# A causal attention and gated FFN layer: K's rows stored once and read through two overlapping windows, and another order for the opening

## The chip, the cores and the metric

The kernel runs on one core of a Trainium2 chip. The metric is the time of one execution in device microseconds. A core has TensorE (PE) for matrix products, VectorE (DVE), ScalarE (ACT) and GpSimd (POOL) for the rest, a sync engine (SP) that only issues transfers here, and 16 DMA engines that carry out what SP, ACT and POOL issue, each through a queue of its own. Data lies in DRAM, in SBUF (128 partitions) or in PSUM, where TensorE writes.

## The reference

Input x is 4096 tokens of 256 features in float32. The layer is attention with its own input norm, a residual and a norm, then the FFN, a residual and a norm:

```python
# attention: 16 heads of 16, causal
xn = (x - mean) * rsqrt(var + 1e-5) * gamma + beta
q, k, v = split(xn @ w_qkv.T)               # w_qkv: (768, 256)
sim = (q * 16**-0.5) @ k.T                  # per head, 4096 x 4096
sim = where(causal_mask, -max, sim)
out = softmax(sim) @ v
x = layernorm(x + out)
# FFN: ternary weights times a scale per output feature
h = silu((x @ w1.T) * s1) * ((x @ w2.T) * s2)    # 256 -> 1024
h = gelu((h @ h1.T) * t1)                        # 1024 -> 1024
h = gelu((h @ h2.T) * t2)                        # 1024 -> 1024
x = layernorm(x + (h @ w3.T) * s3)               # 1024 -> 256
```

## The kernel before

Tokens come in 8 blocks of 512 (`NB`, `B`), heads in 4 groups of four (`NQ`). Precision is kept by splitting: a value is a high part, rounded to the fast format of TensorE, and a low part, the rest. A product of two split values takes high times high, low times high and high times low.

**Projections** (`projections`, L200). For each block of tokens: load x (`fetch`), normalize it, transpose it on TensorE (`front`, L214), split it in xh and xl, and project K, Q and V with the split weights wh and wl, 12 matmuls of 512 columns for K, 12 for Q, 24 of 256 columns for V. The result of K or Q is a tile of 128 output features by 2 by 512 tokens. ACT copies its high part (kh, L263), DVE makes the low part (kl, L265), and both are stored to DRAM (L269): `kaug` and `qaug` hold, for each head, the 16 rows of a part one above another. The tuple `order` says which part goes into each group of 16: K is stored as high, high, low and Q as high, low, high, so that a single product over 48 rows gives the three terms. Two rows of ones (L274) follow in kaug; against them stand, in Q's tile, two rows with the high and low part of the negative row maximum. For block 0 the stores are dealt over the queues of ACT, SP and POOL, for the others they are all POOL's. V goes to `vaug` with a column of ones, which later gives the row sums.

**Attention** (`layer`, L296). Work goes by steps of a query block and a head group. For each step there are two passes over the key blocks up to the diagonal. `row_max` (L425) multiplies Q by K and reduces the maximum of each row on DVE (L453). `rows` (L458) turns these maxima into two rows of Q's tile (qt<-hl, L469). `scores` (L476) multiplies K by Q with all 50 rows, so that the maximum comes off in the product, and ACT takes the exponential (L490). `product` (L500) multiplies V by it; `divide` divides by the row sums and stores the step's output to `attn`.

K is read again for each step and each pass. `fetch(kind, key)` (L401) loads a K tile from kaug, kind "m" (mk) for the maxima, kind "s" (sk, with V in vk) for the scores. Two of each exist, and a tile is asked for one ahead. A K tile takes two loads on SP (L410), half e for partitions 64e to 64e+49, each with two heads side by side:

```python
hs = slice(4 * qd + e, 4 * qd + 4, 2)
nc.sync.dma_start(
    kt[half * e : half * e + KR].bitcast(F32), self.kaug[kb][hs].rearrange("r p t -> p r t")
)
```

**The order of the work.** Each engine's compute instructions run in the order in which the program writes them (`in_order`). A planner writes it: `ahead` gives the row maxima, `behind` the scores; a score step is written when the maxima are `lead` units of work ahead, where `lead` is the size of the current step plus `extra`, and a unit is a quarter of a K tile. After every two or three of them, `other` writes a pair of products, a piece of the projections, or a piece of the FFN. Blocks 0 and 1 are projected before the first step (`FIRST` is 2), the others in between. When all are projected and a query block is finished, its FFN starts (`start`, `feed`): load x and attn, add them, normalize, and run the three layers in pieces with their weights loaded by POOL. The last block's FFN has no attention beside it and comes at the end (`closing`). `scales` loads the FFN's scale vectors, and computes two products of them on POOL; it is called once before the first step.

Of the kernel before, what the change touches and what calls it, by code (L numbers as in the profile page):

```python
# [46 lines left out]

class Layer:
    def __init__(self, tc, a):
        self.tc, self.nc, self.a = tc, tc.nc, a  # L50
        self.last = {}

# [28 lines left out]

    def run(self):
        tc, nc, a = self.tc, self.nc, self.a
        with ExitStack() as ctx:
            dram = self.pool(ctx, "dram", space=DRAM)
            cst = self.pool(ctx, "cst")
            self.small = self.pool(ctx, "small", 4)
            self.qaug = [dram.tile([H, 48, B], F32, name=f"qaug{b}") for b in range(NB)]
            self.kaug = [dram.tile([H, KR, B], F32, name=f"kaug{b}") for b in range(NB)]
            self.vaug = [dram.tile([NQ, P, 4, 4, D + 1], F32, name=f"vaug{b}") for b in range(NB)]  # L90
            self.attn = [dram.tile([B, E], F32, name=f"attn{b}") for b in range(NB)]

# [24 lines left out]
    def scales(self):  # L117
        for n, t in self.sc.items():
            self.nc.sync.dma_start(t, self.a[n].rearrange("(c p) -> p c", p=P))
        self.nc.gpsimd.tensor_scalar(self.w1_half, self.sc["w1_s"], 0.5, None, ALU.mult)  # L120
        self.nc.gpsimd.tensor_tensor(self.w12, self.w1_half, self.sc["w2_s"], ALU.mult)
        s3 = self.a["w3_s"].rearrange("(o f) -> o f", o=1)
        self.nc.sync.dma_start(self.s3, s3.broadcast_to([P, E]))

# [75 lines left out]
    def projections(self, ctx):  # L200
# [7 lines left out]

        def fetch(b):
            xb = wk.tile([P, 4, E], F32, name="xb")  # L210
            nc.sync.dma_start(xb, tokens(a["x"][b * B : (b + 1) * B]))
            return xb

        def front(b, xb):  # L214
            xn = wk.tile([P, 2, B], F32, name="xn", bufs=1)
            for c in range(2):
# [22 lines left out]
        self.layernorm(xb, xb)  # L239
        yield from front(0, xb)  # L240
        xb = ahead
        wh = one.tile([P, 2, 3 * E], FR, name="wh")
        nc.vector.tensor_copy(wh, w)
        wl = one.tile([P, 2, 3 * E], FR, name="wl")
        nc.vector.tensor_tensor(wl, w, wh.bitcast(F32), ALU.subtract)
# [5 lines left out]
        self.layernorm(xb, xb)  # L251
        for b in range(NB):
            xh, xl = parts.pop(b)
            prods = [(wh, xh, c) for c in range(2)] + [(wl, xh, c) for c in range(2)] + [(wh, xl, c) for c in range(2)]
            for off, dst, order in ((E, self.kaug, (0, 0, 1)), (0, self.qaug, (0, 1, 0))):
# [7 lines left out]
                nc.scalar.copy(kh, kp)  # L263
                kl = wk.tile([P, 2, B], FR, name="kl")
                nc.vector.tensor_tensor(kl, kp, kh.bitcast(F32), ALU.subtract)  # L265
                for n, (i, g) in enumerate(sorted((i, g) for g, i in enumerate(order))):
                    for T in range(2):
                        queues = (nc.scalar, nc.sync, nc.gpsimd) if b == 0 else (nc.gpsimd,)
                        queues[(2 * n + T) % len(queues)].dma_start(  # L269
                            dst[b][8 * T : 8 * T + 8, 16 * g : 16 * g + 16, :], (kh, kl)[i][:, T].bitcast(F32)  # L270
                        )
# [24 lines left out]
    def layer(self, ctx):  # L296
# [95 lines left out]
        self.scales()  # L392
# [8 lines left out]
        def fetch(kind, key):  # L401
# [3 lines left out]
            while loaded[kind] < min(j + 2, len(seq)) and seq[loaded[kind]][2] <= self.projected:  # L405
                qb, qd, kb = nxt = seq[loaded[kind]]
                kt = (mk if kind == "m" else sk).tile([P, 2, B], FR, name=kind + "k")
                for e in range(2):
                    hs = slice(4 * qd + e, 4 * qd + 4, 2)
                    nc.sync.dma_start(  # L410
                        kt[half * e : half * e + KR].bitcast(F32), self.kaug[kb][hs].rearrange("r p t -> p r t")
                    )
# [6 lines left out]
                tiles[kind, nxt] = kt, vt  # L419
                loaded[kind] += 1  # L420
# [4 lines left out]
        def row_max(qb, qd):  # L425
            qt = qtile[qb, qd] = qp.tile([P, 2, B], FR, name="qt")
            for e in range(2):
                hs = slice(4 * qd + e, 4 * qd + 4, 2)
                nc.sync.dma_start(
                    qt[half * e : half * e + 48].bitcast(F32), self.qaug[qb][hs].rearrange("r p t -> p r t")  # L430
# [238 lines left out]
    def load(self, b):  # L669
        self.live += 1  # L670
        x1 = self.fk.tile([P, 4, E], F32, name="x1", bufs=3)
        self.nc.sync.dma_start(x1, tokens(self.a["x"][b * B : (b + 1) * B]))
        return x1

    def start(self, b):
# [405 lines left out]
```

## Time and profile before

| | before |
|---|---|
| median of 3 runs | 2464.67 us (2457.7 to 2467.17) |
| the profiled execution | 2476.85 us |
| its span | 2475.1 us |
| mean granted clock of TensorE | 0.933 |
| PE, DVE, ACT, POOL busy | 91%, 63%, 56%, 29% |
| DMA | 310.02 MB in 251,811 packets |

The profile is one execution. It gives, for each engine, the time in which its instructions ran, in total, in 40 slices of the span and by groups of instructions; a group's row names the line, the engine, the operation and its tiles, how often and how long it ran, and what ended the idle time before it. The queue rows count packets: a packet is a piece of a transfer that one DMA engine moves, or a 4-byte completion that it writes when its part of a transfer is done. A window's row gives busy time of PE, PE's weight load, DVE, ACT and POOL, then the granted clock, the mean share of time in which the 16 DMA engines were busy, and GB/s. The chain of waits follows what ended last back to what released it. SPq is SP's queue of issued transfers; in a timeline the second number is how long an issue took.

### The profile page before, as it was taken

The page shows a single profiled execution, that of the slowest core. Times are in us where ns is not written, and L with a number is a line of the kernel's source. Part 1 is how long each engine was busy: PE and PEld are TensorE (multiplying, and loading weights), DVE is VectorE, ACT ScalarE, POOL GpSimd, SP SyncE. Part 2 cuts the span into 40 slices and gives each one's busy share as a digit, 9 for nine tenths or more (in the row PEclk, how much of TensorE's full clock was granted, in tenths as well). Part 3 has the DMA queues.
Part 4 walks back from the last instruction along what each step waited for, and adds up shares of the span by engine and source line. Part 5 has one row for each costly group of instructions (what it writes and reads, how often), then busy time and mean ns, then how long its engine had stood idle before and what let it go on. Part 6 is the DMA issues. An engine that isn't in the chain of part 4 may idle for free.

```text
span 2475.1 us, 36371 instructions
## 1 busy us (share of the span) xinstructions
PE 2259.4 (91%) x13986; PEld 1216.6 (49%) x13986; DVE 1567.3 (63%) x1826; ACT 1394.0 (56%) x1698; POOL 714.2 (29%) x1021
## 2 busy tenths in 40 slices
PE   4677899999998999999899999999999999999888
PEld 3545444545455544545445544554445443454366
DVE  3445687566656667576766677666766467755553
ACT  2242556545655566556665666566666677656731
POOL 2342413143223143131423132131423131313421
PEclk8687889969999989989999989999899999999999
DMA  7776834434643634535354544545354533454933
GB/s 185 200 175 158 192 101 116 121 80 121 128 111 92 156 103 108 129 97 141 103 123 109 139 95 105 132 109 139 80 127 111 142 108 101 110 111 131 243 94 86
DMA packets 251811, 310.02 MB, mean 125 GB/s; under 512 B 41328, under 2 KB 179696, under 8 KB 251632
## 3 DMA queue, kind: packets, MB, share of 16 engines
q1 hardware_dynamic: 141920, 184.87, 26.9%
q0 software_dynamic: 108352, 120.91, 22.6%
q8 instruction: 113, 1.85, 0.3%
q10 hardware_dynamic: 1360, 1.84, 0.2%
q14 instruction: 66, 0.54, 0.1%
HBM read 268.45 MB, written 38.54 MB: 124 GB/s over the span
## 4 chain that ended last, share of the span: by engine, by line
PE 67%; DVE 16%; ACT 7%; DMA 5%; issue 3%; POOL 2%; SPq 0%; ACTq 0%; POOLq 0%; DVEq 0%
PE m L830 17%; PE opsum L504 15%; PE s L486 11%; DVE mp L453 11%; PE s L442 10%; PE m L802 4%; ACT p L490 4%; PE bank L931 2%; PE m L857 2%; PE s L259 2%; PE s L449 1%; DMA qt<-hl 1%; DVE th L806 1%; ACT th L805 1%; DMA mk<-h2T_in 1%
## 5 line engine op out<-in xcount | busy, mean ns | idle before, releaser
L453 DVE TENSOR_REDUCE mp<-s 128x2 f32<-128x1024 f32 (+3 forms) x1152 | 1265.4, 1132 | 560.6 <-PE s L442 404.6
L490 ACT ACTIVATE p<-s 128x1024 f32<-128x1024 f32 (+3 forms) x1152 | 1062.9, 954 | 677.1 <-PE s L486 665.6
L486 PE MATMUL s<-qt,sk 50*128 50x512 f32 (+3 forms) x2304 | 514.6, 452 | 86.2 <-DVE mp L453 46.4
L442 PE MATMUL s<-mk,qt 48*128 48x512 f32 (+3 forms) x2304 | 513.9, 448 | 57.1 <-DVE mp L453 18.4
L504 PE MATMUL opsum<-p,vk 128*17 128x512 f32 (+3 forms) x4608 | 557.0, 586 | 2.8 <-POOL p L493 2.6
L830 PE MATMUL m<-act,wt 128*128 128x512 f32 x1792 | 477.1, 408 | 0.7 <-DVE xl L785 0.7
L486 PEld LDWEIGHTS s<-qt,sk 50*128 50x128 f32 x2304 | 223.1, 193 | 400.5 <-DVE mp L453 141.5
L830 PEld LDWEIGHTS m<-act,wt 128*128 128x128 f32 x1792 | 321.8, 189 | 123.8 <-issue 53.1
L442 PEld LDWEIGHTS s<-mk,qt 48*128 48x128 f32 x2304 | 229.8, 197 | 307.0 <-ACT p L490 134.6
L504 PEld LDWEIGHTS opsum<-p,vk 128*17 128x17 f32 x4608 | 97.7, 98 | 234.1 <-issue 214.1
L493 POOL TENSOR_SCALAR_AFFINE_SELECT p<-p 128x256 f32<-128x256 f32 x256 | 105.1, 420 | 292.1 <-ACT p L490 290.9
L665 POOL DMA_DIRECT2D wt<-h1T_in x64 | 48.9, 764 | 378.9 <-PE m L830 231.0
L665 POOL DMA_DIRECT2D wt<-h2T_in x64 | 49.4, 772 | 366.0 <-PE m L830 310.9
L755 POOL TENSOR_TENSOR act<-raw,act 128x512 fp32r<-128x512 f32 x112 | 145.1, 1295 | 8.9
L838 ACT ACTIVATE raw<-m,h_s 128x512 f32<-128x512 f32 x112 | 77.1, 689 | 107.5 <-PE m L830 107.5
L802 PE MATMUL m<-xh,wt 128*128 128x512 f32 x224 | 105.9, 473 | 11.9 <-DVE th L806 9.1
L449 PEld LDWEIGHTS s<-tri,pick 64*128 64x128 f32 x1024 | 96.1, 205 | 7.2
L802 PE MATMUL m<-xl,wt 128*128 128x512 f32 x224 | 93.3, 416 | 0.0
L449 PE MATMUL s<-tri,pick 64*128 64x128 f32 (+1 forms) x1024 | 88.4, 252 | 0.0
L754 POOL CAST act<-raw 128x512 fp32r<-128x512 f32 x112 | 70.9, 633 | 41.9 <-ACT raw L759 41.9
L754 POOL CAST act<-th 128x512 fp32r<-128x512 f32 x56 | 34.4, 614 | 144.6 <-DVE th L808 144.3
L806 DVE SCALAR_TENSOR_TENSOR th<-th,m 128x512 f32<-128x512 f32 x56 | 38.4, 686 | 55.2 <-ACT th L805 55.1
(126 smaller groups left out, 1530.2 us busy)
## 6 DMA issues: line engine op xcount, KB each, us to landing
mk<-kaug SPq DMA_DIRECT2D x288, 200.0 KB
sk<-kaug SPq DMA_DIRECT2D x288, 200.0 KB
wt<-h1T_in POOLq DMA_DIRECT2D x64, 512.0 KB, 4.3
wt<-h2T_in POOLq DMA_DIRECT2D x64, 512.0 KB, 4.2
vk<-vaug SPq DMA_DIRECT2D x144, 136.0 KB
qt<-qaug SPq DMA_DIRECT2D x64, 192.0 KB
wt<-w1T_in POOLq DMA_DIRECT2D x34, 256.0 KB, 4.2
wt<-w2T_in POOLq DMA_DIRECT2D x34, 256.0 KB, 5.2
```

Source lines behind the costliest of these rows:

```text
L442: nc.tensor.matmul(m[:, e, :k1], qt[rows, r, t * P : (t + 1) * P], kt[rows, r, :k1], start=True, stop=kb != qb,)
L449: nc.tensor.matmul(m[:, e, k1 - P + half * i : k1], pick[rows, i], tri[rows, : P - half * i], start=False, stop=i == 1,)
L453: nc.vector.tensor_reduce(mp[:, r, :, t, kb], m[:, :, :k1], AX.X, ALU.max)
L486: nc.tensor.matmul(s[:, e, lo:], kt[rows, r, t * P : (t + 1) * P], qt[rows, r, lo:], start=True, stop=True)
L490: nc.scalar.activation(p[:, :, lo:], s[:, :, lo:], AF.Exp, scale=0.25)
L493: nc.gpsimd.affine_select(out=p[:, :, lo : lo + P], in_=p[:, :, lo : lo + P], compare_op=ALU.is_ge, fill=0.0, base=0, pattern=[[0, 2], [1, ...
L504: nc.tensor.matmul(opsum[32 * j : 32 * j + D + 1, lo:], vt[:, t, j], pt[j // 2][:, j % 2, lo:], start=first, stop=last,)
L665: self.nc.gpsimd.dma_start(dst, src)
L754: nc.gpsimd.tensor_copy(hi, src)
L755: nc.gpsimd.tensor_tensor(lo, src, hi.bitcast(F32), ALU.subtract)
L802: nc.tensor.matmul(s, wt[:, 2 * i + k, cols], x[:, k], start=k == n == 0, stop=k == n == 1)
L830: nc.tensor.matmul(s, wts[k // 4][:, k % 4, cols], x[:, k % 4], start=k == n == 0, stop=k == 7 and n == 1)
```

## The change

K and Q are stored by dimension: `kaug` becomes 34 rows, each with 16 heads by 512 tokens side by side, `qaug` 48 such rows. K's high part is stored once. Rows 0 to 8 of kaug hold the first 9 rows of the low part, rows 9 to 24 the high part, rows 25 to 31 the rest of the low part, rows 32 and 33 the ones. A load reads rows 0 to 24 and then rows 9 to 33 through an overlapping pattern (`twice`), which gives 50 rows with the high part in them two times; Q's rows are arranged to match. Two heads that share a half of the tile are now neighbours in DRAM, so a row of a load is 4 KB in place of two runs of 2 KB. To get the features of K and Q in this order, their weights are copied by dimension before they are split (`by_dimension`).

The opening changes too. Block 0 of x comes in four loads. The splitting of the weights and the norm steps of blocks 0 and 1 are interleaved in another order. Blocks 0 and 1 are transposed into one PSUM tile of two banks, whose halves ACT and DVE scale. Block 1 is transposed after Q's projection of block 0 in place of K's. Block 0's stores go over the queues of SP and POOL. `scales` is called when the first FFN block starts, and its two products come with that block's addition. `held` orders the loads of x1 and of the scales behind the last K load written so far. `extra` is always 5, where it was 2 for query block 0.

The diff, with what is only declarations left out:

```diff
+KRUNS = ((0, 0, 16, 9), (1, 0, 9, 0), (1, 9, 16, 25))
+QRUNS = ((0, 0, 16, 9), (0, 0, 9, 0), (0, 9, 16, 41), (1, 0, 16, 25))
+
+def twice(ap):
+    dims = [list(d) for d in ap.ap]
+    row = dims[0][0]
+    return bass.AP(ap.tensor, ap.offset, [[9 * row, 2], [row, 25], [1, 2 * B]])
...
+    def held(self):
+        if self.mark:
+            self.after(self.nc.cur_bb.bb.instructions[-1], self.mark)
...
-            self.qaug = [dram.tile([H, 48, B], F32, name=f"qaug{b}") for b in range(NB)]
-            self.kaug = [dram.tile([H, KR, B], F32, name=f"kaug{b}") for b in range(NB)]
+            self.qaug = [dram.tile([48, H, B], F32, name=f"qaug{b}") for b in range(NB)]
+            self.kaug = [dram.tile([34, H, B], F32, name=f"kaug{b}") for b in range(NB)]
...
             self.nc.sync.dma_start(t, self.a[n].rearrange("(c p) -> p c", p=P))
-        self.nc.gpsimd.tensor_scalar(self.w1_half, self.sc["w1_s"], 0.5, None, ALU.mult)
-        self.nc.gpsimd.tensor_tensor(self.w12, self.w1_half, self.sc["w2_s"], ALU.mult)
+            self.held()
...
-            nc.sync.dma_start(xb, tokens(a["x"][b * B : (b + 1) * B]))
+            src = tokens(a["x"][b * B : (b + 1) * B])
+            for ts in [slice(t, t + 1) for t in range(4)] if b == 0 else [slice(0, 4)]:
+                nc.sync.dma_start(xb[:, ts], src[:, ts])
+            loads[b] = nc.cur_bb.bb.instructions[-1].name
...
-            for c in range(2):
+            if b < FIRST:
+                tp = ps.tile([P, 2, B], F32, name="s", tag="s", bufs=3)
+                for t in range(4):
+                    for c in range(2):
+                        nc.tensor.transpose(
+                            tp[:, c, t * P : (t + 1) * P], xb[:, t, c * P : (c + 1) * P], self.ident
+                        )
+                nc.scalar.activation(xn[:, 0], tp[:, 0], AF.Identity, bias=bet[:, 0:1], scale=gam[:, 0:1])
+                nc.vector.tensor_scalar(xn[:, 1], tp[:, 1], gam[:, 1:2], bet[:, 1:2], ALU.mult, ALU.add)
+                yield 8 * TRANSPOSE, True
+            for c in range(2 if b >= FIRST else 0):
...
-        self.layernorm(xb, xb)
+        steps = [step for _, step in self.norm_steps(xb, xb)]
+        for step in steps[:3]:
+            step()
...
+        def by_dimension(copy, off):
+            for k in range(2):
+                for h in range(2):
+                    cs = slice(off + h * P, off + (h + 1) * P)
+                    copy(
+                        wq[:, k, cs].rearrange("p (d q e r) -> p d q e r", d=D, q=2, e=2),
+                        w[:, k, cs].rearrange("p (q r e d) -> p d q e r", d=D, q=2, e=2),
+                    )
+
+        by_dimension(nc.vector.tensor_copy, E)
+        nc.vector.tensor_copy(wh[:, :, E : 2 * E], wq[:, :, E:])
+        for step in steps[3:]:
+            step()
+        by_dimension(nc.scalar.copy, 0)
+        kq = slice(E, 2 * E)
+        nc.vector.tensor_tensor(wl[:, :, kq], wq[:, :, kq], wh[:, :, kq].bitcast(F32), ALU.subtract)
         yield from front(0, xb)
+        for cs, src in ((slice(0, E), wq[:, :, 0:E]), (slice(2 * E, 3 * E), w[:, :, 2 * E :])):
+            nc.vector.tensor_copy(wh[:, :, cs], src)
+            nc.vector.tensor_tensor(wl[:, :, cs], src, wh[:, :, cs].bitcast(F32), ALU.subtract)
...
-                for n, (i, g) in enumerate(sorted((i, g) for g, i in enumerate(order))):
+                for part, d0, d1, row in runs:
                     for T in range(2):
-                        queues = (nc.scalar, nc.sync, nc.gpsimd) if b == 0 else (nc.gpsimd,)
-                        queues[(2 * n + T) % len(queues)].dma_start(
-                            dst[b][8 * T : 8 * T + 8, 16 * g : 16 * g + 16, :], (kh, kl)[i][:, T].bitcast(F32)
+                        queues = (nc.sync, nc.gpsimd) if b == 0 else (nc.gpsimd,)
+                        queues[T % len(queues)].dma_start(
+                            dst[b][row : row + d1 - d0, 8 * T : 8 * T + 8, :],
+                            (kh, kl)[part][8 * d0 : 8 * d1, T].bitcast(F32),
                         )
                 yield 12 * MM, True
                 if dst is self.kaug:
-                    nc.sync.dma_start(self.kaug[b][:, 48:KR, :], ones)
+                    nc.sync.dma_start(self.kaug[b][32:34], ones)
+                    self.after(nc.cur_bb.bb.instructions[-1], loads[b])
+                if dst is (self.kaug if b else self.qaug):
                     if b + 1 < NB:
                         yield from front(b + 1, xb)
...
                 for e in range(2):
-                    hs = slice(4 * qd + e, 4 * qd + 4, 2)
-                    nc.sync.dma_start(
-                        kt[half * e : half * e + KR].bitcast(F32), self.kaug[kb][hs].rearrange("r p t -> p r t")
-                    )
+                    hs = slice(4 * qd + 2 * e, 4 * qd + 2 * e + 2)
+                    nc.sync.dma_start(kt[half * e : half * e + KR].bitcast(F32), twice(self.kaug[kb][:, hs]))
...
+                self.mark = nc.cur_bb.bb.instructions[-1].name
...
-                    qt[half * e : half * e + 48].bitcast(F32), self.qaug[qb][hs].rearrange("r p t -> p r t")
+                    qt[half * e : half * e + 48].bitcast(F32), self.qaug[qb][:, hs].rearrange("p r t -> p (r t)")
...
-                extra = min(EXTRA, 0.8 * size[i])
+                extra = EXTRA
...
+        if b == ORDER[0]:
+            self.scales()
         at = self.fk.tile([P, 4, E], F32, name="at")
...
             nc.gpsimd.tensor_tensor(x1, x1, at, ALU.add)
             self.free("at")
+            if b == ORDER[0]:
+                nc.gpsimd.tensor_scalar(self.w1_half, self.sc["w1_s"], 0.5, None, ALU.mult)
+                nc.gpsimd.tensor_tensor(self.w12, self.w1_half, self.sc["w2_s"], ALU.mult)
```

More of the change, by code (lines that the diff above doesn't have):

```diff
@@ L51, in __init__ @@
         self.last = {}
+        self.mark = None
     def pool(self, ctx, name, bufs=1, **kw):
@@ L119, in scales @@
             self.nc.sync.dma_start(t, self.a[n].rearrange("(c p) -> p c", p=P))
-        self.nc.gpsimd.tensor_scalar(self.w1_half, self.sc["w1_s"], 0.5, None, ALU.mult)
-        self.nc.gpsimd.tensor_tensor(self.w12, self.w1_half, self.sc["w2_s"], ALU.mult)
+            self.held()
         s3 = self.a["w3_s"].rearrange("(o f) -> o f", o=1)
         self.nc.sync.dma_start(self.s3, s3.broadcast_to([P, E]))
+        self.held()
     def norm_steps(self, dst, src):
@@ L207, in projections @@
         wk = self.pool(ctx, "pw", 2, side="right")
+        loads = {}
         def fetch(b):
             xb = wk.tile([P, 4, E], F32, name="xb")
-            nc.sync.dma_start(xb, tokens(a["x"][b * B : (b + 1) * B]))
+            src = tokens(a["x"][b * B : (b + 1) * B])
+            for ts in [slice(t, t + 1) for t in range(4)] if b == 0 else [slice(0, 4)]:
+                nc.sync.dma_start(xb[:, ts], src[:, ts])
+            loads[b] = nc.cur_bb.bb.instructions[-1].name
             return xb
@@ L238, in projections @@
         ahead = fetch(1)
-        self.layernorm(xb, xb)
+        steps = [step for _, step in self.norm_steps(xb, xb)]
+        for step in steps[:3]:
+            step()
+        wq = one.tile([P, 2, 2 * E], F32, name="wq")
+        wh = one.tile([P, 2, 3 * E], FR, name="wh")
+        wl = one.tile([P, 2, 3 * E], FR, name="wl")
+        def by_dimension(copy, off):
[13 more added lines that the diff above has]
+        nc.vector.tensor_tensor(wl[:, :, kq], wq[:, :, kq], wh[:, :, kq].bitcast(F32), ALU.subtract)
         yield from front(0, xb)
+        for cs, src in ((slice(0, E), wq[:, :, 0:E]), (slice(2 * E, 3 * E), w[:, :, 2 * E :])):
+            nc.vector.tensor_copy(wh[:, :, cs], src)
+            nc.vector.tensor_tensor(wl[:, :, cs], src, wh[:, :, cs].bitcast(F32), ALU.subtract)
         xb = ahead
[L242 to L245, printed above, removed]
+        steps = [step for _, step in self.norm_steps(xb, xb)]
+        for step in steps[:4]:
+            step()
         ones = one.tile([32, B], F32, name="ones")
@@ L250, in projections @@
             nc.gpsimd.memset(v, 1.0)
-        self.layernorm(xb, xb)
         for b in range(NB):
@@ L254, in projections @@
             prods = [(wh, xh, c) for c in range(2)] + [(wl, xh, c) for c in range(2)] + [(wh, xl, c) for c in range(2)]
-            for off, dst, order in ((E, self.kaug, (0, 0, 1)), (0, self.qaug, (0, 1, 0))):
+            for off, dst, runs in ((E, self.kaug, KRUNS), (0, self.qaug, QRUNS)):
                 kp = ps.tile([P, 2, B], F32, name="s", tag="s", bufs=3)
@@ L263, in projections @@
                 nc.scalar.copy(kh, kp)
+                if b == 0 and dst is self.kaug:
+                    for step in steps[4:]:
+                        step()
                 kl = wk.tile([P, 2, B], FR, name="kl")
                 nc.vector.tensor_tensor(kl, kp, kh.bitcast(F32), ALU.subtract)
-                for n, (i, g) in enumerate(sorted((i, g) for g, i in enumerate(order))):
+                for part, d0, d1, row in runs:
                     for T in range(2):
-                        queues = (nc.scalar, nc.sync, nc.gpsimd) if b == 0 else (nc.gpsimd,)
-                        queues[(2 * n + T) % len(queues)].dma_start(
-                            dst[b][8 * T : 8 * T + 8, 16 * g : 16 * g + 16, :], (kh, kl)[i][:, T].bitcast(F32)
+                        queues = (nc.sync, nc.gpsimd) if b == 0 else (nc.gpsimd,)
+                        queues[T % len(queues)].dma_start(
+                            dst[b][row : row + d1 - d0, 8 * T : 8 * T + 8, :],
+                            (kh, kl)[part][8 * d0 : 8 * d1, T].bitcast(F32),
                         )
@@ L391, in layer @@
         nc.vector.memset(opsum, 0.0)
-        self.scales()
         steps = [(qb, qd) for qb in ORDER for qd in range(NQ)]
@@ L427, in row_max @@
             for e in range(2):
-                hs = slice(4 * qd + e, 4 * qd + 4, 2)
+                hs = slice(4 * qd + 2 * e, 4 * qd + 2 * e + 2)
                 nc.sync.dma_start(
-                    qt[half * e : half * e + 48].bitcast(F32), self.qaug[qb][hs].rearrange("r p t -> p r t")
+                    qt[half * e : half * e + 48].bitcast(F32), self.qaug[qb][:, hs].rearrange("p r t -> p (r t)")
                 )
@@ L672, in load @@
         self.nc.sync.dma_start(x1, tokens(self.a["x"][b * B : (b + 1) * B]))
+        self.held()
         return x1
```

## The prediction, made before the changed kernel ran

> **What bounds the kernel now.** I read the page first (spans, slices, queues), then the windows table, then what the K tiles wait for, and last the opening as a timeline of SP.
>
> ```profile
> span 2475.1 us, 36371 instructions
> PE 2259.4 (91%) x13986; PEld 1216.6 (49%) x13986; DVE 1567.3 (63%) x1826; ACT 1394.0 (56%) x1698; POOL 714.2 (29%) x1021
> ...
> PE   4677899999998999999899999999999999999888
> ...
> PEclk8687889969999989989999989999899999999999
> DMA  7776834434643634535354544545354533454933
> ```
>
> PE is busy in nine tenths of nearly every slice after the sixth and in 4 to 8 tenths before, at a lower clock. So there are two parts: a body that TensorE bounds, and an opening of about 300 us with room in it.
>
> ```profile
> 300.00:2200.00 1900.00, 1804.56 (x11410) 927.08 (x11406) 1280.18 (x1373) 1153.41 (x1357) 530.01 (x729) 0.95 0.46 114
> 2350.00:2475.00 125.00, 101.98 (x504) 80.21 (x502) 53.36 (x108) 30.96 (x46) 26.89 (x35) 0.93 0.35 89
> ```
>
> From 300 to 2200 us PE is busy 95% at clock 0.95, while the 16 DMA engines are busy 0.46 of the time on average: the transfers are hidden. How well shows in what the score matmuls' tile waited for:
>
> ```profile
>   DMA sk<-kaug: 3.8, 4
> ```
>
> 3.8 us in four waits, in the whole run. Now how those hidden transfers are spread:
>
> ```profile
> q1 hardware_dynamic: 141920, 184.87, 26.9%
> q0 software_dynamic: 108352, 120.91, 22.6%
> ...
> q10 hardware_dynamic: 1360, 1.84, 0.2%
> ...
> mk<-kaug SPq DMA_DIRECT2D x288, 200.0 KB
> sk<-kaug SPq DMA_DIRECT2D x288, 200.0 KB
> vk<-vaug SPq DMA_DIRECT2D x144, 136.0 KB
> qt<-qaug SPq DMA_DIRECT2D x64, 192.0 KB
> ```
>
> K is by far the largest traffic: 576 loads of 200 KB are 118 MB of the 310 MB. A K tile takes two loads (partitions 0 to 49 and 64 to 113), so there are 144 tiles for the maxima (mk) and 144 for the scores (sk), one of each every 2295/144 = 15.9 us between the first load (46 us) and the last (2341 us), and every 14 us in the body.
>
> The opening has one stall to see, on SP:
>
> ```profile
> 46.34 0.33 SPq L410 DMA_DIRECT2D mk<-kaug  x1
> 46.72 3.11 SPq L269 DMA_DIRECT2D qaug<-kl  x1
> 49.88 4.77 SPq L410 DMA_DIRECT2D mk<-kaug  x2
> 62.33 0.96 SPq L429 DMA_DIRECT2D qt<-qaug  x2
> ```
>
> A store of Q's low part stands in SP's order behind a K load that had to wait for K's stores. It leaves at 46.7 though its data was there at about 36; the chain of waits then shows 15.53 us of qaug<-kl and 5.81 us of qt<-qaug, and the first maxima matmul (L442) runs at 67.9 us.
>
> **The change, part by part.**
>
> *The K load.* Before, each load reads 50 rows x 2 heads, 100 runs of 2 KB. After, `twice` reads 2 windows x 25 rows, 50 runs of 4 KB. Bytes and the number of loads stay the same. Packets get longer: in the trace's packet records a 2 KB packet on SP's queue takes 87 ns (median), the 3 KB ones of wqkv 121 ns, the 4 KB ones of the stores 159 ns. That is 23.5 against 25.8 bytes per ns, so 9% less engine time, all of it hidden.
>
> The other thing that changes is the outermost dimension of the source: 50 before, 2 after. What that does can be read in the queue rows, because each DMA engine that a load uses adds one 4-byte completion packet. ACT's queue (q10): 1360 packets, of which 1280 are data (256 of wqkv, 2 x 256 of gam and bet, 4 stores x 128); 80 are left. Three loads with 128 rows at 16 make 48, so each of the four stores, 128 partitions into 8 heads, has 8. Its outer sizes are 128 and 8, and it runs on 8 engines. SP's queue (q1): 130,176 of its 141,920 packets are data (64,512 of 2 KB, 27,776 of 1 KB, 18,432 of vk, 14,336 of attn, 1,024 of hl, 4,096 single scales), 11,744 are completions. Everything but K comes to 5,984, with 16 for transfers of 128, 48 or 32 rows and 8 for the stores by head and the four-kilobyte qt<-hl. That leaves 5,760, exactly 10 for each of the 576 K loads of 50 rows. This is the rule of the Trainium skill (DMA: Bandwidth & Descriptors, "Why a DMA increments its semaphore by 16 and not by 1"): a DMA runs on the largest number of engines up to 16 that divides the outermost size of both sides. It fits these rows to the packet, and it speaks against this change: 2 and 50 have only 2 in common. The page's "Rules for kernel authors" says that a leading dimension of c copies confines the DMA to c engines, and that a load from SP takes the lowest-numbered ones; no row here shows which they are, but if so, all K loads share the same two.
>
> The sum by the rule: 25 packets per engine x 159 ns = 3.98 us a load, 7.95 us a tile (before: 20 packets x 87 ns = 1.74 us on ten), 576 x 3.98 = 2290 us of work for two engines. By bytes alone, spread as before, it is 576 x 5 x 159 ns = 458 us each on ten, hidden as today.
>
> Those two engines also carry their sixteenth of the rest. All queues together show 50.1% of 16 x 2475 us, 1240 us per engine; K is 57,600 packets x 115 ns mean / 16 = 414 of it, which leaves 826 us. That contains packets waiting for each other; at the undisturbed median of each size it is 625 us. About 80 us of either lies before the first K load or after the last. So 545 to 745 us fall into the K window; I take 640. 2290 + 640 = 2930 us of work, for a window of 2295 us: the two engines become the bound. Tile by tile: 15.9 + about 4 = 20 us for a pair that PE now finishes in about 14.
>
> What waits: the first maxima matmul or score matmul on a new tile. PE runs in program order, so the products, the FFN matmuls and the transposes stand behind it, then the maxima on DVE, the exponentials on ACT and the FFN's splits on POOL. Only two tiles of each kind are held, so no earlier issue helps. Behind K's packets in SP's rings stand vk, qt and qt<-hl, which need the same two engines.
>
> *Stores.* K is written in 32 rows a head instead of 48, Q in 48 as before: 0.5 MB less a block, 4.2 MB of 310 in all. DMAs: 6 for K as before, 8 instead of 6 for Q. At 0.6 us of POOL each that is 1.2 us a block, 8 to 10 us in all, on an engine busy 29%; cover gone, that much. In block 0 ACT's queue is no longer used, which frees some 4 us of ACT.
>
> *The weights by dimension.* Eight copies of 128x128 with a strided read, which the trace does not show. Nearest rows: ACT's 128x256 copy 370 ns, DVE's 128x512 cast about 0.35 us from wh's 0.95 for 1536. So 0.2 to 0.4 us each: about 1 us on DVE ahead of the first mean shift and 1.2 on ACT ahead of the first xn; 1 to 2.5 us on the opening's path, since DVE is then in order behind wqkv's landing. The cast and subtraction of weights (2.7 us) are the same work, split so that K's third comes first; that returns up to 2 us.
>
> *The opening's order.* x of block 0 in four loads (3 more SP issues, 0.4 us each), so that statistics start before the whole 6.4 us load: 0 to 3 us gained. Block 1's transposes come after Q's projection, and Q's stores no longer wait behind K's load: 10 to 20 us of the 21 us stall above. The lead at query block 0 becomes 5 instead of 2 tiles of work: of the three waits for qt<-hl in the chain (8.24, 9.01, 9.80 us) it can touch only the first, 0 to 8 us.
>
> *The scales.* Four loads and s3 leave SP's opening (1.83 to 10.1 us, 8.2 us of issue, with nothing urgent behind them but the ones' stores) and come when the first FFN block starts; K loads of the body then queue behind 8 us of SP: 0 to 8 us. The two small POOL instructions that use them (0.2 us each) move along and are hidden behind the seven turns that the addition is deferred. The ordering that holds x1 and the scales behind the last K load adds no instruction.
>
> With K spread as before the middles sum to -15 us, the ends to -32 and, if nothing gained in the opening reaches the end, +8.
>
> **The sum.** 46 us to the first K load + 2930 + 132 us (2343 to 2475, the closing FFN without K) = 3108 us. I add 1 to 2% for moments in which the two engines run dry, as when SP stands at a store of attn or at qt<-hl (the waits for hl in SP's own table are 97 us now): about 3160. PE's work fits in: 2259 us of busy time in 3160. The profiled execution took 2476.85 us, 12 over the median; brought to the median, **3150**. Ends: at the 27 GiB/s per engine of the same page's "Specifications" (an estimate of 141 ns a packet, which no row here reaches) 2030 + 545 + 178 = 2750; at 745 us of other traffic, with 5% idle and a PE clock that falls to the opening's 0.8, about 3420.
>
> **Rivals.**
> - *K stays spread over ten engines or more* (the two windows reach the queue as 50 rows). For it: the SBUF side still counts 50 rows. Against it: the four stores with 128 on one side and 8 on the other ran on 8. Then the opening's gain remains: 2465 - 15 = 2450 us, faster. It is decided by the number of engines alone: with three, 4580/3 + 640 = 2167 us still fits into the 2295 us window; with two it does not.
> - *Two engines, mostly hidden*: packets overlap within an engine, or the rest avoids these two. Near 120 ns a packet 1730 + 545 us just fits; in between it gives 2500 to 2860, say 2750. Against it: bursts of one K load (100 packets) never take under 1.18 us, where ten engines with packets in a row need 0.87.
> - *Nothing*: only hidden transfers and idle engines change, and the stall in the opening comes back at the next wait: 2465.
>
> **How the numbers follow.** About 0.5% (12 us) is what a measurement of this kernel can tell from no change. Two engines as the bound: 0.80, at 3150 with its own range 2880 to 3420. Two engines, partly hidden: 0.08. Spread, faster: 0.09. Nothing: 0.03. Slower by over 0.5%: 0.80 + 0.08 = 0.88; faster 0.09; same 0.03. The range 2840 to 3420 leaves out the last two cases, half of the second and some 3% above.
>
> **What would show it.** Right: SP's packets fall by 28,800 in data and by 4,608 completions (576 x 8) and hardly change otherwise; "DMA mk<-kaug" and "sk<-kaug" head the waits of PE and of the chain; PE's busy share is near 72 to 75% in every slice, its clock below 0.95; the mean DMA share falls while the time rises; a pair of tiles every 20 us. Wrong: K loads with 10 or more completions each, PE still at 95% in the body, and a first maxima matmul near 50 us; then the time is the opening's alone.

## The result and the profile after

The changed kernel takes 3151.76 us (median of 4 runs, 3150.25 to 3158.85), the kernel before 2465.92 us beside it: a ratio of 1.2769, 95% interval 1.2731 to 1.2806. It is slower by 28%. The profiled execution took 3150.46 us.

The page of the changed kernel, cut to spans and slices, queues, shares of the chain of waits, and the two groups of matmuls that read K tiles (L502 for the maxima, L546 for the scores):

```profile
span 3148.6 us, 36435 instructions
...
PE 2530.2 (80%) x13986; PEld 1344.9 (43%) x13986; DVE 1579.7 (50%) x1836; ACT 1402.1 (45%) x1700; POOL 719.4 (23%) x1038
...
PE   6677788888888788887888878787888877888768
...
PEclk8786678888898888897889888888888977888889
DMA  5455234342243333333233332333233332233633
...
q1 hardware_dynamic: 105664, 185.12, 17.9%
q0 software_dynamic: 104080, 117.48, 17.5%
...
DMA 52%; PE 31%; DVE 5%; issue 3%; SPq 2%; ACT 2%; POOL 1%; POOLq 0%; DVEq 0%; ACTq 0%
DMA mk<-kaug 23%; DMA sk<-kaug 21%; PE opsum L564 7%; PE m L896 7%; PE s L546 5%; PE s L502 5%; DVE mp L513 3%; DMA vk<-vaug 3%; PE m L868 2%; PE bank L997 2%; SPq L471 1%; PE m L923 1%; DMA mk<-h1T_in 1%; DMA mk<-h2T_in 1%; DMA qt<-hl 1%
...
L502 PE MATMUL s<-mk,qt 48*128 48x512 f32 (+3 forms) x2304 | 606.3, 484 | 257.2 <-DMA mk<-kaug 191.1
L546 PE MATMUL s<-qt,sk 50*128 50x512 f32 (+3 forms) x2304 | 590.4, 481 | 260.0 <-DMA sk<-kaug 196.0
```

The last two kinds of line read before:

```profile
PE 67%; DVE 16%; ACT 7%; DMA 5%; issue 3%; POOL 2%; SPq 0%; ACTq 0%; POOLq 0%; DVEq 0%
...
L486 PE MATMUL s<-qt,sk 50*128 50x512 f32 (+3 forms) x2304 | 514.6, 452 | 86.2 <-DVE mp L453 46.4
L442 PE MATMUL s<-mk,qt 48*128 48x512 f32 (+3 forms) x2304 | 513.9, 448 | 57.1 <-DVE mp L453 18.4
```

The chain was 67% PE and 5% DMA, and is now 52% DMA, 44 points of it K tiles. Yet the row "DMA" in tenths is lower than before: 16 engines are idler on average while the kernel waits for them. The window that carries it, after:

```profile
300.00:2200.00 1900.00, 1566.70 (x8700) 805.71 (x8699) 994.23 (x1071) 877.31 (x1037) 416.19 (x582) 0.84 0.33 89
```

PE is busy 1567 us of 1900 (before 1805), at a granted clock of 0.84 (0.95), and the DMA share is 0.33 (0.46). The time lost can be split: the span grew by 673.5 us; PE's idle time grew from 216 to 618 us, and its busy time from 2259 to 2530 us for the same 13,986 matmuls. The mean granted clock explains the second part: it fell from 0.933 to 0.833, and 2259 x 0.933 / 0.833 is 2530. In the runs below it falls in step with the waiting (0.942 for two loads of 25, 0.907 for a half, 0.874 for three quarters); that the waiting causes it is my reading, which no run tests by itself.

The queue rows say why. Of SP's 105,664 packets 98,432 are data and 7,232 completions. The SP transfers besides K now have 6,080 (5,984 before, + 48 for three more loads of x, + 48 for block 0's stores, which have 16, 9 and 7 engines for 16, 9 and 7 dimensions). That leaves 1,152: two for each of the 576 K loads.

The trace's packet records show the same in another way. In the body, from 300 to 2200 us, 4 KB packets of SP's queue are in flight for 95% of the time: exactly two for 76%, one for 13%, three or more for 5% (Q's tiles, which use more engines, are among them). In the kernels below, the number in flight for the most time is 5 for two loads of 25 rows, 10 for 50 rows and 3 for 51 rows. Two K loads leave SP within 1.3 us, and each needs about 4 us on two engines (an estimate: 25 packets of 162 ns). On different pairs of engines they would show four in flight; four to twelve are seen for 1% of the time. So the loads share the same two.

From the view of the tile sk, the issue of its loads on SP (ns, least, median and most) and what its matmuls and weight loads waited for (us, times):

```profile
L471 SPq DMA_DIRECT2D sk<-kaug x288: 587/588/8915, 65.3 to 3011.0; - x144
...
  DMA sk<-kaug: 358.5, 117
```

3.8 us in four waits have become 358.5 in 117. SP itself is held up, up to 8.9 us for one issue. The body on SP, as a timeline (start, how long the issues took):

```profile
1614.87 1.24 SPq L471 DMA_DIRECT2D sk<-kaug  x2
1617.82 3.62 SPq L471 DMA_DIRECT2D mk<-kaug  x2
1621.53 0.38 SPq L475 DMA_DIRECT2D vk<-vaug  x1
1635.25 1.25 SPq L471 DMA_DIRECT2D sk<-kaug  x2
1638.19 2.60 SPq L471 DMA_DIRECT2D mk<-kaug  x2
```

A pair of K tiles every 20.4 us; before it was every 14. And the opening, where the change did what it says:

```profile
30.62 1.26 SPq L328 DMA_DIRECT2D qaug<-kl  x1
31.98 1.31 SPq L233 DMA_DIRECT2D xb<-x_in  x1
33.41 1.10 SPq L471 DMA_DIRECT2D mk<-kaug  x1
37.69 0.80 SPq L489 DMA_DIRECT2D qt<-qaug  x2
```

Q's last store leaves at 30.6 us, ahead of the first K load and not behind it (46.7 before), and the first maxima matmul runs at 48.9 us in place of 67.9. The opening gains 19 us there and the body loses nearly 700.

### The profile page after: what moved, and what is told of

It reads as the page before. It is cut to its first block, busy times and chain, and to the rows that moved or that the text cites. A ratio compares the mean times of both kernels' runs of the same rounds, so it can differ in the third digit from the quotient of the medians.

```text
span 3148.6 us, 36435 instructions
## 1 busy us (share of the span) xinstructions
PE 2530.2 (80%) x13986; PEld 1344.9 (43%) x13986; DVE 1579.7 (50%) x1836; ACT 1402.1 (45%) x1700; POOL 719.4 (23%) x1038
## 3 DMA queue, kind: packets, MB, share of 16 engines
q1 hardware_dynamic: 105664, 185.12, 17.9%
## 4 chain that ended last, share of the span: by engine, by line
DMA 52%; PE 31%; DVE 5%; issue 3%; SPq 2%; ACT 2%; POOL 1%; POOLq 0%; DVEq 0%; ACTq 0%
DMA mk<-kaug 23%; DMA sk<-kaug 21%; PE opsum L564 7%; PE m L896 7%; PE s L546 5%; PE s L502 5%; DVE mp L513 3%; DMA vk<-vaug 3%; PE m L868 2%; PE bank L997 2%; SPq L471 1%; PE m L923 1%; DMA mk<-h1T_in 1%; DMA mk<-h2T_in 1%; DMA qt<-hl 1%
## 5 line engine op out<-in xcount | busy, mean ns | idle before, releaser
L502 PE MATMUL s<-mk,qt 48*128 48x512 f32 (+3 forms) x2304 | 606.3, 484 | 257.2 <-DMA mk<-kaug 191.1
L546 PE MATMUL s<-qt,sk 50*128 50x512 f32 (+3 forms) x2304 | 590.4, 481 | 260.0 <-DMA sk<-kaug 196.0
L564 PE MATMUL opsum<-p,vk 128*17 128x512 f32 (+3 forms) x4608 | 615.2, 637 | 25.8 <-DMA vk<-vaug 18.6
L896 PE MATMUL m<-act,wt 128*128 128x512 f32 x1792 | 527.7, 441 | 6.1 <-POOL act L821 3.0
L546 PEld LDWEIGHTS s<-qt,sk 50*128 50x128 f32 x2304 | 261.6, 210 | 602.8 <-issue 203.5
L502 PEld LDWEIGHTS s<-mk,qt 48*128 48x128 f32 x2304 | 273.7, 215 | 564.7 <-DMA mk<-kaug 169.8
L896 PEld LDWEIGHTS m<-act,wt 128*128 128x128 f32 x1792 | 353.8, 208 | 148.9 <-issue 61.8
L509 PEld LDWEIGHTS s<-tri,pick 64*128 64x128 f32 x1024 | 118.3, 243 | 13.4 <-DVE tri L451 5.8
L868 PE MATMUL m<-xh,wt 128*128 128x512 f32 x224 | 117.3, 524 | 6.0 <-DVE th L872 4.7
L509 PE MATMUL s<-tri,pick 64*128 64x64 f32 (+1 forms) x1024 | 106.4, 282 | 5.6 <-DVE tri L451 5.6
## 6 DMA issues: line engine op xcount, KB each, us to landing
wt<-h1T_in POOLq DMA_DIRECT2D x64, 512.0 KB, 11.5
```

Source lines behind the costliest of these rows:

```text
L502: nc.tensor.matmul(m[:, e, :k1], qt[rows, r, t * P : (t + 1) * P], kt[rows, r, :k1], start=True, stop=kb != qb,)
L509: nc.tensor.matmul(m[:, e, k1 - P + half * i : k1], pick[rows, i], tri[rows, : P - half * i], start=False, stop=i == 1,)
L546: nc.tensor.matmul(s[:, e, lo:], kt[rows, r, t * P : (t + 1) * P], qt[rows, r, lo:], start=True, stop=True)
L564: nc.tensor.matmul(opsum[32 * j : 32 * j + D + 1, lo:], vt[:, t, j], pt[j // 2][:, j % 2, lo:], start=first, stop=last,)
L868: nc.tensor.matmul(s, wt[:, 2 * i + k, cols], x[:, k], start=k == n == 0, stop=k == n == 1)
L896: nc.tensor.matmul(s, wts[k // 4][:, k % 4, cols], x[:, k % 4], start=k == n == 0, stop=k == 7 and n == 1)
```

## The experiments

The theory: a K load runs on two DMA engines because its source counts 2 in its outermost dimension, the two are always the same, and their work sets the time. The rivals: the wide rows are slow (1), the overlap is (2), the new opening or SP's order is (3). The first four kernels tell these apart. The kernel with the gap, three quarters, both halves and three engines ran twice each, the others 4 to 22 times; the kernel before, beside them, took 2468.5 to 2469.8 us in the median.

**Two loads of 25 rows.** The same rows in DRAM, the same overlap, the same 4 KB packets; only the pattern is taken apart:

```diff
-                    nc.sync.dma_start(kt[half * e : half * e + KR].bitcast(F32), twice(self.kaug[kb][:, hs]))
+                    for g in range(2):
+                        r0 = half * e + 25 * g
+                        nc.sync.dma_start(
+                            kt[r0 : r0 + 25].bitcast(F32),
+                            self.kaug[kb][9 * g : 9 * g + 25, hs].rearrange("p r t -> p (r t)"),
+                        )
```

> The changed kernel, but each K load through the overlapping pattern is replaced by two loads of 25 rows (rows 0 to 24, rows 9 to 33). Same rows in DRAM, same 4 KB runs, same packets; twice as many loads (1152). Theory (two engines): 25 rows against 25 partitions run on 5 engines, 28,800 packets x 162 ns / 5 = 933 us + some 640 us of other traffic = 1573 us, well under the K window, so K is hidden again and only the opening's gain is left: 2450 us (2430 to 2475). Rival 1 (wide rows or their 32 KB pitch in DRAM are slow whatever the engines): about 3100 us. Rival 2 (the overlap: the same rows read twice in a short time): about 3100 us, since the overlap stays. Rival 3 (the new opening or SP's order is what costs): about 3100 us.

Measured: 2471.64 us, ratio to the kernel before 1.0015 (0.9991 to 1.0039). 680 us are gone with this edit alone, so rivals 1, 2 and 3 fall: rows, overlap, opening and most of SP's order are as in the changed kernel. Its queue row and its wait:

```profile
q1 hardware_dynamic: 110272, 185.14, 24.0%
```

```profile
  DMA sk<-kaug: 7.1, 6
```

4,608 packets more than the changed kernel, with the same data: 1152 loads x 5 completions less 576 x 2. But the opening's gain does not show in the time; that is taken up below.

**K stored twice, loaded as 50 rows, and the same with a gap.** The second version differs from the first by one unused row in DRAM, which makes of 50 rows 2 groups of 25 (the size of `kaug` and the place of its ones, which follow, are left out):

```diff
 # 50 rows
-KRUNS = ((0, 0, 16, 9), (1, 0, 9, 0), (1, 9, 16, 25))
+KRUNS = ((0, 0, 16, 9), (0, 0, 16, 25), (1, 0, 9, 0), (1, 9, 16, 41))
...
-twice(self.kaug[kb][:, hs])
+self.kaug[kb][:, hs].rearrange("p r t -> p (r t)")
 # with a gap, against the 50 rows
-KRUNS = ((0, 0, 16, 9), (0, 0, 16, 25), (1, 0, 9, 0), (1, 9, 16, 41))
+KRUNS = ((0, 0, 16, 9), (0, 0, 16, 26), (1, 0, 9, 0), (1, 9, 16, 42))
...
-self.kaug[kb][:, hs].rearrange("p r t -> p (r t)")
+twice(self.kaug[kb][:, hs])   # now [[26 * row, 2], [row, 25], [1, 2 * B]]
```

> The changed kernel, but K's high part is stored twice (kaug has 50 rows of 16 heads) and a K load reads 50 rows of 4 KB in one pattern. Theory (two engines): 50 against 50 runs on 10 engines, 28,800 x 162 ns / 10 = 467 us + 640 us, hidden: 2450 us (2430 to 2475), the same as the two loads of 25 within 0.5%; K's stores are 4.2 MB more again, 0 to 5 us. Rival 1 (wide rows): about 3100 us. Rival 2 (the overlap): 2450 us as well. Rival 3 (opening): about 3100 us.

> As the kernel with K's high part stored twice, but with one unused row in DRAM between rows 24 and 25 of the 50, so that a load is again 2 groups of 25 rows, now without any overlap. Nothing else differs from the 50-row version. Theory (two engines): the outermost size is 2 again, 2290 to 2330 us of packets for two engines: 3150 us (3100 to 3200), DMA completions of K loads 2 each. Rival 2 (the overlap): 2450 us, as nothing is read twice. Rivals 1 and 3: about 3100 us, with the 50-row version just as slow.

Measured: 2457.9 us in 50 rows (0.9954, 0.9935 to 0.9972), 3161.71 us with the gap (1.2796, 1.2723 to 1.2869). Nothing is read twice here, and the time is that of the changed kernel again. The queue row of the 50 rows, then that of the gap, then the gap's wait for score tiles:

```profile
q1 hardware_dynamic: 110416, 185.40, 27.7%
```

```profile
q1 hardware_dynamic: 105808, 185.38, 18.0%
```

```profile
  DMA sk<-kaug: 365.0, 112
```

The difference is 4,608 packets, 576 loads x 8 completions: ten engines against two. Both kernels store the same data in the same order and read each row once, so rivals 1 to 3 can't make this difference. A pattern in two groups also takes SP longer to issue (a median of 0.59 us against 0.33), which this pair does not take apart from the engines. The packets in flight do (two here as well, for 76% of the body), and so do the three engines below, with a plain pattern that SP issues in 0.29 us.

**Three quarters and a half.** With only some of the loads through the overlapping pattern and the others as two loads of 25:

```diff
+                    if kind == "m" or e == 0:     # three quarters; a half: kind == "s"
+                        nc.sync.dma_start(kt[half * e : half * e + KR].bitcast(F32), twice(self.kaug[kb][:, hs]))
+                        continue
```

> The changed kernel, but of the four K loads of a pair of tiles the second half of the score tile (sk, partitions 64 to 113) goes as two loads of 25 rows, the other three stay as they are. The sum of the prediction, with 162 ns a packet: 432 loads x 25 x 162 ns = 1750 us on the two engines, + 1440 x 162 ns = 233 us as their fifth of the rest of K, + 640 us other traffic = 2623 us, + 46 + 132 us outside the K window = 2800 us (2720 to 2900). If the two engines alternated among more than one pair, or if any one such load is enough to stall a tile for as long as now, the time would be near 2460 us or near 3100 us.

> The changed kernel, but the maxima's K tiles (mk) go as two loads of 25 rows each half, and only the scores' (sk) through the overlapping pattern. Sum with 162 ns: 288 x 25 x 162 = 1166 us on the two engines, + 14,400 x 162 / 5 = 467 us, + 640 us = 2273 us for a K window of about 2280: it just fits. By the sum alone about 2460 us. With three quarters the measured time was 54 us over the sum, so bursts and dry moments count: I expect 2500 us (2465 to 2560). If the time simply went with the share of K loads on two engines, 2471.6 at none and 3152 at all, it would be 2812 us.

Measured: 2853.86 us for three quarters (1.155, 1.1483 to 1.1617) and 2670.0 us for a half (1.0807, 1.0773 to 1.0841). The first lies in the expected range, 54 us over the sum. The second is a miss: 210 us over the sum, and outside what I expected; nor is it the 2812 us of a time that goes with the share of loads. Half of K is on the two engines, and the kernel still waits:

```profile
  DMA sk<-kaug: 150.9, 52
```

So the total work of the busiest engines, which predicts the full case well, says too little when it is near the window (here 2273 us, where K loads on ten engines take 2282 us from first to last).

**The same half, dealt otherwise.** The first half of every tile through the overlapping pattern, in place of every second tile (`if e == 0`). The sum for the two engines is the same.

> The changed kernel with half of K on two engines, as before, but dealt otherwise: the first half (partitions 0 to 49) of every tile through the overlapping pattern, the second half as two loads of 25 rows. The sum for the two engines is the same 2273 us. If their total work sets the time: 2670 us as in the other half (2640 to 2700). If it is that a score tile alone holds the two engines for 8 us and keeps what stands behind it waiting, each tile now holds them for 4 us and the time falls: 2500 to 2620 us.

Measured: 2590.34 us (1.0478, 1.0419 to 1.0538), 80 us less at the same sum, and the score tiles wait less:

```profile
  DMA sk<-kaug: 41.0, 26
```

How long one tile holds the two engines counts beside how much they have to do. My reading, which this pair supports but does not prove: with two tiles of each kind, a load has little more than one tile's time to land, and a score tile on two engines takes 8 us out of 14, with what else stands in their rings.

**Three engines.** The 50-row version, with a 51st row of ones in DRAM that is loaded and that no product reads (one small store more a block):

```diff
-kt[half * e : half * e + KR].bitcast(F32), self.kaug
+kt[half * e : half * e + KR + 1].bitcast(F32), self.kaug
```

> The version with K stored twice and loaded in 50 rows (10 engines, 2457.9 us), but with one row more, of ones, that is loaded too and that no product reads: 51 rows against 51 partitions leave 3 as the largest divisor up to 16. 17 packets x 162 ns x 576 loads = 1586 us on three engines + 640 us = 2226 us. The prediction held that three engines still fit, since 2167 (here 2226) is under the window of about 2290 us: then 2460 us (2450 to 2500). The kernel with half of K on two engines had a sum of 2273 us and took 2670 us, its engines busy for 91% of its K window. If that is general: 2226 / 0.91 + 178 = 2624 us (2560 to 2680).

Measured: 2604.9 us (1.0537, 1.048 to 1.0594), where ten engines took 2457.9. The prediction's remark that three engines would fit is wrong; the estimate from the half version (2624) is near. One row more in a load costs 6%, through the divisor. Its queue row, then what its score tiles waited for:

```profile
q1 hardware_dynamic: 107216, 188.01, 23.0%
```

```profile
  DMA sk<-kaug: 86.3, 40
```

Of these packets 99,264 are data (576 more than with 50 rows for the row itself, 128 for its stores) and 7,952 completions. Other transfers have 6,224 (the 6,080 of the changed kernel, 16 for K's second high part in block 0, 128 for the stores of the row), which leaves 1,728, three for each K load.

Put together, with 162 ns a packet and 640 us of other traffic as in the prediction, against the time from the first to the last issue of a K load in each profile:

| K loads | sum for the busiest engines | K window | share | time |
|---|---|---|---|---|
| 50 rows, 10 engines | 1107 us | 2282 us | 0.49 | 2458 us |
| two of 25, 5 engines | 1573 | 2302 | 0.68 | 2472 |
| 51 rows, 3 engines | 2226 | 2431 | 0.92 | 2605 |
| half of each tile on 2 | 2273 | 2412 | 0.94 | 2590 |
| score tiles on 2 | 2273 | 2498 | 0.91 | 2670 |
| three quarters on 2 | 2623 | 2688 | 0.98 | 2854 |
| all on 2 (the change) | 2973 | 2978 | 1.00 | 3152 |

The more of the work is on them, the closer the busiest engines come to being busy all the time; at nine tenths the kernel loses 5 to 8% already. But the K window of this table is each run's own, which the waiting has lengthened. Of the 2282 us that ten engines leave, 2226 and 2273 us are 0.98 and 1.00. And the 640 us is uncertain: in the K windows of the changed kernel, of three engines and of the score tiles on two, the packets of all other transfers come to 570 to 585 us per engine at the median of each size and to 750 to 780 us as recorded, if they are spread evenly. With the upper figure, these three middle sums lie above 2282 us.

**Five engines against twelve.** Two experiments on the 14 us between the two loads of 25 and the 50 rows. In the changed kernel, windows of 24 and 26 rows, with the low part cut 8 and 8:

```diff
-KRUNS = ((0, 0, 16, 9), (1, 0, 9, 0), (1, 9, 16, 25))
-QRUNS = ((0, 0, 16, 9), (0, 0, 9, 0), (0, 9, 16, 41), (1, 0, 16, 25))
+KRUNS = ((0, 0, 16, 8), (1, 0, 8, 0), (1, 8, 16, 24))
+QRUNS = ((0, 0, 16, 8), (0, 0, 8, 0), (0, 8, 16, 40), (1, 0, 16, 24))
...
+                    for r0, n, row in ((0, 24, 0), (24, 26, 8)):
+                        nc.sync.dma_start(
+                            kt[half * e + r0 : half * e + r0 + n].bitcast(F32),
+                            self.kaug[kb][row : row + n, hs].rearrange("p r t -> p (r t)"),
+                        )
```

> K's high part stored once, and each K load as two loads again, but with windows of 24 rows (0 to 23) and 26 rows (8 to 33), for which the low part's dimensions are cut 8 and 8 in place of 9 and 7. 24 rows can use 12 engines and 26 rows 13, where two loads of 25 used 5. The two loads of 25 took 2471.6 us, the 50-row version 2457.9. If the five engines were what cost those 14 us: 28,800 x 162 ns / 12.5 = 373 us, and about 2455 us (2448 to 2462), since K's stores are also smaller. If the doubled number of loads on SP was: about 2471 us (2464 to 2480).

Measured: 2460.55 us (0.9964, 0.9947 to 0.9981), against 1.0015 (0.9991 to 1.0039) for two loads of 25. Its queue row:

```profile
q1 hardware_dynamic: 118912, 185.17, 27.6%
```

That is 8,640 more than with two loads of 25, 576 x (12 + 13 - 10). As many loads, 11 us less: the engines cost it, not the number of issues. (The stores of the low part are cut otherwise too, 8 and 8 in place of 9 and 7; that was not tested by itself.) K's high part is stored once here and the opening's gain shows. In the kernel before, its loads taken apart into two of 25 rows:

```diff
-                    nc.sync.dma_start(
-                        kt[half * e : half * e + KR].bitcast(F32), self.kaug[kb][hs].rearrange("r p t -> p r t")
-                    )
+                    for g in range(2):
+                        r0 = half * e + 25 * g
+                        nc.sync.dma_start(
+                            kt[r0 : r0 + 25].bitcast(F32),
+                            self.kaug[kb][hs, 25 * g : 25 * g + 25].rearrange("r p t -> p r t"),
+                        )
```

> The kernel before, with each K load as two loads of 25 rows and nothing else changed: 5 engines in place of 10, twice as many loads. 57,600 packets of 2 KB x 87 ns / 5 = 1002 us + 640 us = 1642 us, 72% of the K window. If five engines are few enough to be felt, as the two loads of 25 in the changed kernel suggest against windows of 24 and 26 (11 us), 2480 us (2472 to 2490). If K is fully hidden at that share, 2469 us (2462 to 2474).

Measured: 2493.51 us (1.0074, 1.003 to 1.0118). Its interval does not hold 1, so two loads of 25 cost time without any other part of the change. Whether the five engines do, or twice as many loads, this run can't tell; the one before speaks for the engines. The median of its five runs lies above the expected range; the sign is clear, the size is not.

**Parts of the opening.** Both on the 50-row version. The lead at query block 0 as before, and the scales loaded before the first step as before (their two products on POOL move back with them):

```diff
 # lead
-                extra = EXTRA
+                extra = min(EXTRA, 0.8 * size[i])
 # scales
         nc.vector.memset(opsum, 0.0)
+        self.scales()
...
-        if b == ORDER[0]:
-            self.scales()
```

> The version with K stored twice and loaded in 50 rows (2457.9 us), with the lead at query block 0 as it was before the change (extra = min(EXTRA, 0.8 * size)). The prediction gave this edit 0 to 8 us: 2458 to 2466 us; if the longer lead was worth nothing or cost something, 2450 to 2458.

> The version with K stored twice and loaded in 50 rows (2457.9 us), with the scales loaded and multiplied before the first attention step as before the change. In the opening they put 8 us of issues back on SP and POOL's two products behind them; in the body they no longer stand in front of K loads. The prediction gave the move 0 to 8 us of cost in the body and no gain in the opening: 2450 to 2458 us. If SP's opening is tight now, 2458 to 2470 us.

Measured: 2462.9 us with the old lead (0.9977, 0.9962 to 0.9991) and 2452.44 us with early scales (0.992, 0.9895 to 0.9946), against 2457.9 us (0.9954, 0.9935 to 0.9972). Each moves 5 us in the expected direction, and the intervals overlap: neither is shown by itself.

**The best version.** Windows of 24 and 26 rows and early scales together:

> The changed kernel with two edits that the runs point to: windows of 24 and 26 rows (12 and 13 engines, 2460.6 us) and the scales loaded ahead of the first step as before the change (2452.4 against 2457.9 us in the 50-row version). If both add up: 2453 us (2445 to 2460), faster than both kernels by 0.5 to 0.8% of the kernel before. If the scales' gain belonged to the other version's order alone: 2460 us.

Measured: 2456.23 us (0.995, 0.9931 to 0.9969). It is faster than the kernel before by half a per cent, and 695 us faster than the changed kernel, with K's high part still stored once. Early scales move it by 4 us against the 24 and 26 rows alone, the same way as in the other pair. The 50 rows with early scales have the lowest median of all, 2452.44 us; the intervals of the two overlap.

## Why the prediction was right, and where it was not

**The engine count**: two completions for each K load, as the rule gave it, and with a gap row in place of the overlap the same. The Trainium skill's rule (DMA: Bandwidth & Descriptors, "Why a DMA increments its semaphore by 16 and not by 1") held for 50, 25, 2 x 25, 51, 24 and 26 rows: 10, 5, 2 and 3 completions a load, and 25 for the last two together. Which engines they are no run shows; that it is the lowest-numbered ones stands in that same section, not in "Rules for kernel authors", where I put it. That all loads share the same two is shown by the packets in flight, and the time agrees: dealt over two pairs in turn, an engine would have 1167 + 640 = 1807 us, between the five engines (1573 us, a time of 2472) and the three (2226 us, 2605), far from 3152.

**The sum**: 46 + 2930 + 132 us, and 1 to 2% for dry moments. By the profile: the first K load is issued at 33 us (the opening's gain, which that sum left out), the last at 3011, and 138 us follow. In the window of 2978 us the two engines have 2973 us to do at a median of 162 ns a packet, 3 ns more than the row that I took. So 13 us less at the start, 43 more for the packets, 6 more at the end, and by the sum only 5 us for dry moments in place of 52: terms that were off in both directions and cancelled. Nor do the dry moments follow from the sum alone: no K packet is in flight for 5% of the body, and what the two engines do then isn't recorded. The 12 us that I took off, because the profiled execution before lay over its median, has no counterpart after (3150.46 against 3151.76), and made up for the 10 us that were left. That the time came out within 2 us is luck to that extent. The 640 us was chosen in the middle of 545 to 745, and the window bounds it only from above.

**PE**: I expected 72 to 75% busy in every slice, and it is 80%. The term that failed is the clock: it fell to 0.833 in the mean (0.84 in the body), which makes the same work 2530 us in place of 2259. I had said only that it would be below 0.95, and used a lower one in the sum only at the upper end. By the engines' sum, which fills the window without it, it cost no time of its own; no run tests that.

**The rivals**: that three engines would still fit, and that two would nearly hide at 120 ns a packet, rested on comparing a sum with a window. The step that failed is that a sum just under the window means hidden: 2226 us on three engines took 2605 us. With the other traffic uncertain by some 100 us, the sum was not even sure to be under it; and the two halves, 80 us apart at the same sum, show that how the work is dealt over the tiles counts too.

**The opening**: the middles summed to -15 us with K spread. The 50-row version gained 12 us (0.9954), with K stored twice; the first maxima matmul came 20 us earlier in it, at 48.1 us. The copies by dimension took 253 ns on DVE and 399 ns on ACT, in the 0.2 to 0.4 us that I gave them. Lead and scales came out with the expected sign, each about as large as can be measured.

**Packets**: I said that SP's packets would fall by 28,800 in data. They fell by 31,744. I left out Q's tiles, whose 6,144 runs of 2 KB became 3,072 of 4 KB; 128 more came from block 0's stores.

## What to carry to other kernels

Before giving a load a pattern with a small outer dimension, count how many engines it will run on; the completions in the queue rows of a profile tell it for the loads that are there, and a mean DMA share says nothing about the busiest engine. Two loads with a good divisor on both sides can be far faster than one with a clever pattern. A transfer is hidden when each of its pieces lands in the time that its buffers leave, not when its total just fits into the span: here engines whose work came, by the sum, to 0.98 to 1.00 of the window cost 5 to 8%, and 0.69 of it cost half a per cent.

## What the runs showed of the hardware beyond that

- The issue of a K load on SP took a median of 0.59 us with the pattern of two groups, against 0.33 in the 50-row version and 0.30 for 25 rows. In the half version both kinds stand side by side: 0.61 us for two groups, 0.29 for 25 rows. It is not simply the number of engines, since 51 rows on three engines took 0.29 us. The longest issue took 8.9 us, in which SP issues nothing else.
- The 4 KB packets of SP's queue took 179 ns in the mean with K on two engines, 189 on three, 194 on five and 232 in the 50-row version on ten. With fewer engines each packet is faster, but not nearly in proportion.
- The loads of the FFN's weights h1 by POOL, the same as before, took 11.5 us to land in place of 4.3; 9.0 with K on three engines, 5.0 on five and 4.2 on ten. That a part of each stands behind K's packets on the few engines is the likely reason; no record shows it.
